# Reordering the prologue of a fused adaLN block: fewer products of zeros, statistics first, part of the normalisation on GpSimd

## The chip, the cores and the metric

The kernel runs on one core of a Trainium2 chip. The metric is the time of one execution on the device, in microseconds. The engines are TensorE (PE; its weight loads are PEld), VectorE (DVE), ScalarE (ACT), GpSimd (POOL) and SyncE (SP), which issues most DMAs.

## The reference

For 8 batches x of 1024 rows by 256 columns, in float32:

```python
mod = (_silu(L0_c) @ L0_wmod).reshape(8, 6, 1, -1)
sa, ca, ga, sb, cb, gb = (mod[:, i] for i in range(6))
ga = (2 * (ga >= 0) - 1) * jnp.maximum(jnp.abs(ga), 0.25)     # gb likewise
h = _layernorm(x) * (1 + ca) + sa
x = x + ga * attention(h)       # softmax((h * w_lhs) @ (h * w_rhs).T) @ h
h = _layernorm(x) * (1 + cb) + sb
x = x + gb * (relu(h @ W1 + b1) @ W2 + b2)
```

The weights are 256 by 1536 (wmod), 256 by 1024 (W1) and 1024 by 256 (W2). The scores of one batch are symmetric up to the two sides w_lhs and w_rhs, which the kernel folds into per-column scales and shifts.

## The kernel before, in words

A batch has eight row tiles of 128 (NT), in two halves g of four (TH). The program is one long list of instructions. Every engine runs its own part of the list strictly in the order in which it was written: the function pin() at the end ties each instruction to the one before it on its engine, so the order of the calls in the source is the order of the queues. Engines wait for each other through semaphores.

The prologue (lines 79 to 167, 923 to 1051) prepares batch 0. After it, the loop over batches and row tiles (from line 1135) interleaves attention of batch b with the feed-forward part of batch b-1. TensorE does nearly all of that.

In the prologue:

- Loads. c, the rows of x of batch 0 in four pieces of two tiles (load_x0), wmod in two pieces (its first 512 columns on ScalarE's queue, the other 1024 on SP's), w_lhs and w_rhs, the biases, and x of batch 1.
- warm(n), line 138: one product of zeros with n columns on TensorE. One of 512 columns stands ahead of the transposes of c, and two of 512 and one of 256 stand behind them.
- SiLU of c, lines 157 to 164: two small transposes into pt, exp(-c) on ScalarE (den), then three VectorE instructions that make scT.
- mod_rows(part, parts), line 185: product of scT and a stretch of wmod (pmr), copied to rows by ScalarE (L197). mod_rows(0, 2) makes shift and scale of the attention, mod_rows(2, 1) and mod_rows(5, 1) the two gates.
- columns(wv, NI), line 171: w_lhs and w_rhs as columns (pt_v, L175). make_sides, line 215, transposes shift and scale into columns (pmc, L206) and multiplies them with those of w (four small VectorE instructions, L218 and L221).
- prepare_stats, prepare_rstd, prepare_norm (lines 256 to 285): mean and variance of a tile (two VectorE instructions, L237 and L238), 1/sqrt as exp(-0.5 log) (two on ScalarE, L243 and L244, for a half), and x normalised into xg (VectorE for batch 0, L282, one instruction for each tile).
- prepare_turn(0, g), line 343: eight transposes on TensorE (pth, L355; four tiles into each of two PSUM tiles), from which lT and rT, the two sides with their scale and shift, are made: lT on VectorE for the first half (L359) and on ScalarE for the second (vector=False, L369), rT on ScalarE (L363). The pool ps_t has two PSUM buffers, used in turn by all transposes.
- direct(0, i, parts), line 397: scores of row tile i (psc, L405) with one half of the columns, copied to sc by ScalarE (L412). direct(0, 0) and direct(0, 1) start with the first half of the columns, which need rT of the first half alone.
- Then the gates (lines 943 to 953, eight VectorE instructions on 8 partitions), their way to DRAM (rows_d), the loads of W1 and W2 behind them on SP, first_rows (prow, L992), keep_rows (L1002), the gate's multiplication of xg (xg_half, L1020), maxima and mirrored score blocks (mirror_first, L444 and L445).

Before the change the calls stand in this order: statistics of half 0, its rstd, mod_rows(0, 2), columns, two tiles' statistics of half 1, normalisation of half 0, the other two tiles' statistics, make_sides, prepare_turn(0, 0), rstd of half 1, its normalisation, the gates' mod_rows, prepare_turn(0, 1), direct(0, 0), direct(0, 1).

Of the kernel before, what the change touches and what calls it, by code (L numbers as in the profile page):

```python
# [11 lines left out]
F32 = mybir.dt.float32  # L12
AF = mybir.ActivationFunctionType
ALU = mybir.AluOpType
# [3 lines left out]
P = 128  # L18
# [6 lines left out]
def adaln_block_kernel(  # L25
# [13 lines left out]
    nc = tc.nc  # L39
    B, S, D = x.shape  # L40
# [4 lines left out]
    HALF = 512  # L45
    TH = HALF // P
# [10 lines left out]
    ps_t = ctx.enter_context(tc.tile_pool(name="ps_t", bufs=2, space=PSUM))  # L57
# [37 lines left out]
    c_sb, b2_row = early_d[:B, 0], early_d[:B, 1]  # L95
# [36 lines left out]
    ident = const.tile([P, P], F32, name="ident")  # L132
# [5 lines left out]
    def warm(n):  # L138

        pw = ps_s.tile([P, HALF], F32, tag="s", name=f"pw_{n}")  # L140
        nc.tensor.matmul(pw[:, :n], lhsT=zeros[:, :P], rhs=zeros[:, :n], start=True, stop=True)
# [6 lines left out]
            name=nc.get_next_instruction_name(),  # L148
            engine=mybir.EngineType.Activation,
# [1 line left out]
    )  # L151

    warm(HALF)
    pt = ps_t.tile([P, HALF], F32, tag="t", name="pt_c")
    NC_ = ND * B
    for k in range(ND):
        nc.tensor.transpose(pt[:, ts(k, B)], c_sb[:, ts(k, P)], ident[:B, :B])
    scT = const.tile([P, ND, B], F32, name="scT")
    scf = scT.rearrange("p k b -> p (k b)")
    den = const.tile([P, NC_], F32, name="den")  # L160
    nc.scalar.activation(den, pt[:, :NC_], AF.Exp, scale=-1.0)
    nc.vector.tensor_scalar(den, den, 1.0, None, ALU.add)
    nc.vector.reciprocal(den, den)
    nc.vector.tensor_tensor(scf, pt[:, :NC_], den, ALU.mult)
    warm(HALF)
    warm(HALF)
    warm(D)

# [16 lines left out]
    def mod_rows(part, parts):  # L185

        pm = ps_a.tile([P, HALF], F32, tag="a", name=f"pmr_{part}")
        w = parts * D
        for k in range(ND):
            nc.tensor.matmul(  # L190
                pm[:B, :w],
                lhsT=scT[:, k, :],
                rhs=wm[:, k, ds(part * D, w)],
                start=(k == 0),
                stop=(k == ND - 1),
            )
        nc.scalar.copy(  # L197
            mod[:, part : part + parts, :].rearrange("b s d -> b (s d)"), pm[:B, :w]
        )
# [13 lines left out]
    side_col = lambda side, what, k, b: sides[:, side, what, k, b : b + 1]  # L213

    def make_sides():
        pc = mod_columns(0)
        for side in range(2):
            nc.vector.scalar_tensor_tensor(  # L218
                sides[:, side, 0], pc[:, 1], 1.0, w_cols(side), ALU.add, ALU.mult
            )  # L220
            nc.vector.tensor_tensor(sides[:, side, 1], pc[:, 0], w_cols(side), ALU.mult)  # L221
# [5 lines left out]
    def rows_tile(b):  # L227
        rows_t[b] = two.tile([P, 2, D], F32, tag="rows", name=f"rows_{b}")
        return rows_t[b]
# [5 lines left out]
    def stats(mv, t, src, name):  # L235
        st = work.tile([P, nc.vector.BN_STATS_DIM], F32, tag="st", name=f"st_{name}")
        nc.vector.bn_stats(st, src)  # L237
        nc.vector.bn_aggr(mv[:, t, :], st)  # L238
# [13 lines left out]
    def prepare_start(b):  # L252
        xg_t[b] = two.tile([P, NT, DX], F32, tag="xg", name=f"xg_{b}")
        nc.gpsimd.memset(xg_t[b][:, :, D : D + 1], 1.0)

    def prepare_stats(b, g, tiles=range(TH)):

        if tiles[0] == 0:
            mv = work.tile([P, TH, 2], F32, tag="mva", name=f"mva_{b}_{g}")
            pre[b, g] = [mv]  # L260
        mv = pre[b, g][0]
        for j in tiles:
            stats(mv, j, x_t[b, g][:, j, :], f"a{b}_{g}_{j}")

    def prepare_rstd(b, g):
        pre[b, g].append(rstd_of(pre[b, g][0], "ra", f"ra_{b}_{g}"))

    def prepare_norm(b, g):

        mv, r = pre.pop((b, g))  # L270
        if b > 0:
            shift = work.tile([P, TH], F32, tag="rs", name=f"rs_{b}_{g}")
            nc.vector.scalar_tensor_tensor(shift, mv[:, :, 0], -1.0, r, ALU.mult, ALU.mult)
        for j in range(TH):
            t = g * TH + j
            if b > 0:
                nc.scalar.activation(
                    xg_t[b][:, t, 0:D], x_tile(b, t), AF.Identity,
                    scale=r[:, j : j + 1], bias=shift[:, j : j + 1],
                )  # L280
                continue
            nc.vector.tensor_scalar(  # L282
                xg_t[b][:, t, 0:D], x_tile(b, t), mv[:, j, 0:1], r[:, j : j + 1],
                ALU.subtract, ALU.mult,
            )
# [57 lines left out]
    def prepare_turn(b, g, vector=True):  # L343

        xg, pts = xg_t[b], []
        lT = lT_t[b, g] = two.tile([P, ND, HALF], F32, tag="lT", name=f"lT_{b}_{g}", bufs=2)
        rT = rT_t[b, g] = two.tile([P, ND, HALF], F32, tag="rT", name=f"rT_{b}_{g}", bufs=2)
        rows = lambda T, k: T[:, k, :].rearrange("p (t a v) -> p t a v", a=NV, v=V)
        for k in range(ND):
            if b > 0:  # L350
                pt = pre[b, g][:, k]
            else:
                pt = ps_t.tile([P, HALF], F32, tag="t", name=f"pth_{b}_{g}_{k}")
                for j in range(TH):
                    nc.tensor.transpose(pt[:, ts(j, P)], xg[:, g * TH + j, ts(k, P)], ident)  # L355
                pt = pt.rearrange("p (t a v) -> p t a v", a=NV, v=V)
            pts.append(pt)
            if vector:
                nc.vector.tensor_scalar(  # L359
                    rows(lT, k), pt, side_col(0, 0, k, b), side_col(0, 1, k, b),  # L360
                    ALU.mult, ALU.add,
                )
            nc.scalar.activation(  # L363
                rows(rT, k), pt, AF.Identity,
                scale=side_col(1, 0, k, b), bias=side_col(1, 1, k, b),
            )
        if not vector:
            for k in range(ND):
                nc.scalar.activation(  # L369
                    rows(lT, k), pts[k], AF.Identity,  # L370
                    scale=side_col(0, 0, k, b), bias=side_col(0, 1, k, b),
                )

# [10 lines left out]
    def score_row(b, i):  # L386
        if b == 0:
            return first_scores()[:, i].rearrange("p (n v) -> p n v", v=V)
        return sc_t[b].rearrange("p i a j v -> p j (i a) v")[:, i]
# [6 lines left out]
    def direct(b, i, parts=range(S // HALF)):  # L396
        if i == 0 and parts[0] == 0:
            sc_t[b] = two.tile([P, NT, NV, NT, V], F32, tag="sc", name=f"sc_{b}", bufs=1)
        for n in parts:
            lo, hi = max(i * P, n * HALF), (n + 1) * HALF  # L400
            if lo >= hi:
                continue
            psc = ps_s.tile([P, HALF], F32, tag="s", name=f"psc_{b}_{i}_{n}")
            for k in range(ND):
                nc.tensor.matmul(  # L405
                    psc[:, : hi - lo],
                    lhsT=lT_t[b, i // TH][:, k, ts(i % TH, P)],
                    rhs=rT_t[b, n][:, k, lo - n * HALF : HALF],
                    start=(k == 0),
                    stop=(k == ND - 1),  # L410
                )
            nc.scalar.copy(  # L412
                score_row(b, i)[:, lo // V : hi // V, :],
                psc[:, : hi - lo].rearrange("p (n v) -> p n v", v=V),
            )
# [505 lines left out]


    prepare_start(0)
    prepare_stats(0, 0)
    prepare_rstd(0, 0)
    mod_rows(0, 2)
    columns(wv, NI)
    prepare_stats(0, 1, range(2))
    prepare_norm(0, 0)
    prepare_stats(0, 1, range(2, TH))  # L930
    make_sides()
    prepare_turn(0, 0)
    prepare_rstd(0, 1)
    prepare_norm(0, 1)
    mod_rows(2, 1)
    mod_rows(5, 1)
    prepare_turn(0, 1, vector=False)
    direct(0, 0, range(1))
    direct(0, 1, range(1))


# [11 lines left out]
    nc.vector.tensor_tensor(rows_sb[:, 3, :], gate[:, 1, :], b2_row, ALU.mult)  # L953


    rows_tile(0)
    rows_d = dram.tile([B, 4, D], F32, name="rows_d")
    nc.sync.dma_start(out=rows_d, in_=rows_sb)
# [369 lines left out]
    b = B - 1  # L1328
# [75 lines left out]
```

## Time and profile before

| what | value |
|---|---|
| runs | 776.5, 776.8, 777.04 us, median 776.8 |
| the profiled execution | 778.43 us |
| its span (first to last instruction) | 776.6 us |
| TensorE busy | 762.5 us, 98% of the span |
| VectorE, ScalarE, GpSimd busy | 74%, 47%, 69% |
| granted TensorE clock over the span | 1.0 |
| first 24 us: TensorE busy | 21.18 us |
| first 24 us: VectorE, ScalarE, GpSimd busy | 14.08, 9.88, 1.72 us |

The page lists the chain of work that ended last: followed back from the last instruction, at each step to what released it, or to the instruction before it on its engine. The same chain can be listed in order of time for a stretch. The timeline lists each instruction with start, duration, engine, line, the tile written and the tile read, and in square brackets how long its engine had been idle before it and which instruction ended that. A float32 product shows as two rows, one for each of two passes. DMA issues come with the time from issue to landing.

### The profile page before, as it was taken

To read this page: it belongs to the slowest core of one execution; us is meant where nothing else is said; L and a number is where in the kernel's file an instruction comes from. 1 tells how busy PE (TensorE), PEld (TensorE's weight loads), DVE (VectorE), ACT (ScalarE), POOL (GpSimd) and SP (SyncE) were. 2 spreads that over 40 slices of the span, in tenths; PEclk is the share of its full clock that TensorE was granted. 3 is DMA by queue.
4 is the path that set the end of the run, shared out by engine and by line. 5 is a ranking of instruction groups with operands and counts; after the bars stand their busy time and mean duration, and the time that the engine had idled before them with its cause. 6 is when DMAs were issued, how large, how long until landed. Compare 5 with 4: busy or idle time off the path is not lost.

```text
span 776.6 us, 11486 instructions
## 1 busy us (share of the span) xinstructions
PE 762.5 (98%) x3710; PEld 620.6 (80%) x3710; DVE 575.8 (74%) x1238; ACT 366.4 (47%) x671; POOL 534.0 (69%) x626
## 2 busy tenths in 40 slices
PE   8999999999999999999999999999999999999998
PEld 3576788788887888878887888878888788889886
DVE  6597879768796787957888677876879677594632
ACT  4464545535465355544546444553546535251511
POOL 0533895977949688586868778497694968559641
PEclk9999999999999999999999999999999999999999
DMA  5314434355344464434543544435444335232220
GB/s 190 124 28 149 123 103 119 122 167 169 95 128 126 130 177 113 144 104 125 169 126 116 150 149 129 110 121 177 139 121 125 107 122 170 58 103 86 81 82 27
DMA packets 106211, 95.18 MB, mean 123 GB/s; under 512 B 29700, under 2 KB 98848, under 8 KB 106152
## 3 DMA queue, kind: packets, MB, share of 16 engines
q1 hardware_dynamic: 98408, 85.81, 37.8%
q10 hardware_dynamic: 7744, 8.65, 3.5%
q8 instruction: 29, 0.48, 0.2%
q14 instruction: 30, 0.25, 0.1%
HBM read 50.62 MB, written 43.81 MB: 122 GB/s over the span
## 4 chain that ended last, share of the span: by engine, by line
PE 84%; DVE 10%; issue 2%; ACT 2%; POOL 1%; DMA 1%; SPq 0%; DVEq 0%; POOLq 0%
PE psc L405 14%; PE po L488 13%; PE pa L713 8%; PE pb L713 6%; PE yb L791 6%; PE ya L791 6%; PE pc L713 6%; PE yc L791 5%; PE pr L579 4%; PE pp L539 3%; PE py L896 3%; PE pq L579 3%; PE yd L791 3%; DVE pT L467 1%; DVE m L455 1%
## 5 line engine op out<-in xcount | busy, mean ns | idle before, releaser
L765 POOL TENSOR_TENSOR f<-f,kept 128x512 f32<-128x512 f32 x64 | 81.7, 1276 | 118.2 <-DVE f L764 89.6
L405 PE MATMUL psc<-rT,lT 128*128 128x512 f32 (+3 forms) x384 | 134.3, 486 | 0.0
L488 PE MATMUL po<-xg,pT 128*128 128x257 f32 x576 | 131.6, 380 | 0.0
L488 PEld LDWEIGHTS po<-xg,pT 128*128 128x128 f32 x576 | 108.8, 190 | 16.0 <-issue 1.0
L405 PEld LDWEIGHTS psc<-rT,lT 128*128 128x128 f32 x384 | 67.6, 190 | 38.1 <-issue 27.0
L412 ACT COPY sc<-psc 128x512 f32<-128x512 f32 (+3 forms) x96 | 44.8, 474 | 96.5 <-PE psc L405 96.5
L467 DVE TENSOR_TENSOR pT<-sc,pm 128x1024 f32<-128x1024 f32 x64 | 77.1, 1205 | 5.9 <-PE pm L460 5.8
L774 ACT ACTIVATE f<-f 128x512 f32<-128x512 f32 x64 | 40.4, 631 | 83.8 <-POOL f L765 83.8
L476 ACT ACTIVATE pT<-pT 128x1024 f32<-128x1024 f32 x64 | 67.0, 1047 | 26.4 <-DVE pT L467 26.4
L455 DVE TENSOR_REDUCE m<-sc 128x1 f32<-128x1024 f32 x64 | 77.1, 1205 | 0.0
L732 ACT COPY kept<-pa 128x512 f32<-128x512 f32 x64 | 37.4, 585 | 80.7 <-PE pa L713 80.7
L629 POOL TENSOR_TENSOR x<-x,rows 128x256 f32<-128x256 f32 x64 | 45.3, 740 | 37.4 <-ACT rows L1002 23.2
L713 PE MATMUL pb<-hs,w1s 128*128 128x256 f32 x256 | 67.1, 385 | 0.9 <-DVE f L750 0.6
L713 PE MATMUL pc<-hT,w 128*128 128x256 f32 x256 | 66.2, 381 | 0.0
L428 DVE STREAM_TRANSPOSE Tm<-sc 128x896 f32<-128x896 f32 (+6 forms) x49 | 34.7, 707 | 27.6 <-ACT sc L412 27.3
L713 PEld LDWEIGHTS pc<-hT,w 128*128 128x128 f32 x256 | 48.1, 190 | 7.7 <-ACT kept L732 1.4
L713 PEld LDWEIGHTS pb<-hs,w1s 128*128 128x128 f32 x256 | 45.5, 191 | 11.0 <-DVE f L750 4.6
L791 PE MATMUL yc<-f,w2s 128*128 128x256 f32 x224 | 52.1, 379 | 0.0
L791 PEld LDWEIGHTS yc<-f,w2s 128*128 128x128 f32 x224 | 41.5, 190 | 10.1 <-issue 2.9
L786 POOL TENSOR_TENSOR ft<-ft,f 128x256 f32<-128x256 f32 x56 | 41.9, 749 | 4.4
L785 POOL TENSOR_TENSOR ft<-ft,f 128x256 f32<-128x256 f32 x56 | 40.9, 730 | 4.4
L861 POOL TENSOR_TENSOR x<-x,Y 128x512 f32<-128x512 f32 x28 | 35.0, 1272 | 10.6 <-DMA Y<-D_y 10.6
(164 smaller groups left out, 1676.2 us busy)
## 6 DMA issues: line engine op xcount, KB each, us to landing
D_f<-T_f SPq DMA_DIRECT2D x60, 128.0 KB, 2.3
X_f<-D_f SPq DMA_DIRECT2D x15, 512.0 KB, 3.9
D_a<-T_a SPq DMA_DIRECT2D x56, 128.0 KB, 3.5
D_y<-T_y SPq DMA_DIRECT2D x56, 128.0 KB, 2.8
Y<-D_y SPq DMA_DIRECT2D x14, 512.0 KB, 3.9
out_dram<-x SPq DMA_DIRECT2D x14, 512.0 KB, 4.3
X_a<-D_a SPq DMA_DIRECT2D x13, 512.0 KB, 3.4
x<-in_L_attn_x_dram ACTq DMA_DIRECT2D x12, 512.0 KB, 3.8
```

Source lines behind the costliest of these rows:

```text
L405: nc.tensor.matmul(psc[:, : hi - lo], lhsT=lT_t[b, i // TH][:, k, ts(i % TH, P)], rhs=rT_t[b, n][:, k, lo - n * HALF : HALF], start=(k == ...
L412: nc.scalar.copy(score_row(b, i)[:, lo // V : hi // V, :], psc[:, : hi - lo].rearrange("p (n v) -> p n v", v=V),)
L455: nc.vector.tensor_reduce(m, score_row(b, i), AX.XY, ALU.max)
L467: nc.vector.tensor_tensor(pT.rearrange("p j (a v) -> p j a v", v=V), score_columns(b, i), pm[:, :P].rearrange("p (j a v) -> p j a v", j=1, ...
L476: nc.scalar.activation(pT_t[b, i], pT_t[b, i], AF.Exp)
L488: nc.tensor.matmul(po[:, : D + 1], lhsT=pT[:, t, :], rhs=xg_t[b][:, t, 0 : D + 1], start=(t == 0), stop=(t == NT - 1),)
L579: nc.tensor.matmul(out, lhsT=lhs[:, t, :], rhs=rhs[:, t, :], start=(t == 0), stop=(t == TH - 1),)
L629: queue.append(lambda: nc.gpsimd.tensor_tensor(out, in0, row, op))
L713: nc.tensor.matmul(out, lhsT=lhsT, rhs=rhs, start=True, stop=True)
L765: nc.gpsimd.tensor_tensor(f[:, c::NH, hi], f[:, c::NH, hi], kept[:, None, hi].to_broadcast([P, 2, H2]), ALU.add,)
L786: add(ft[:, 2, c], ft[:, 1, c], f[:, c + NH, lo], ALU.subtract)
L791: nc.tensor.matmul(out, lhsT=lhs(c), rhs=rhs(c), start=(c == 0), stop=(c == NH - 1))
```

## The change

The call of warm(512) behind the transposes of c is left out once (two of 512 and one of 256 become one of each). The three VectorE instructions of SiLU are put into a function, which is called behind the statistics of the first two tiles. Normalisation of batch 0 goes to GpSimd for every tile from the third on (t counts over all eight, so that is two tiles of the first half and all four of the second). The rstd and the normalisation of the second half stand ahead of prepare_turn(0, 0). direct(0, 0) with the first half of the columns stands ahead of prepare_turn(0, 1). The lT of the second half is made on VectorE and not on ScalarE, by the function left, which is called behind the gates. No load is moved.

```diff
     warm(HALF)
...
-    nc.vector.tensor_scalar(den, den, 1.0, None, ALU.add)
-    nc.vector.reciprocal(den, den)
-    nc.vector.tensor_tensor(scf, pt[:, :NC_], den, ALU.mult)
-    warm(HALF)
+
+    def silu():
+        nc.vector.tensor_scalar(den, den, 1.0, None, ALU.add)
+        nc.vector.reciprocal(den, den)
+        nc.vector.tensor_tensor(scf, pt_c[:, :NC_], den, ALU.mult)
+
     warm(HALF)
     warm(D)
...
-            nc.vector.tensor_scalar(
+            engine = nc.vector if t < TH // 2 else nc.gpsimd
+            engine.tensor_scalar(
                 xg_t[b][:, t, 0:D], x_tile(b, t), mv[:, j, 0:1], r[:, j : j + 1],
                 ALU.subtract, ALU.mult,
             )
...
-        if not vector:
+        def left():
             for k in range(ND):
-                nc.scalar.activation(
-                    rows(lT, k), pts[k], AF.Identity,
-                    scale=side_col(0, 0, k, b), bias=side_col(0, 1, k, b),
+                nc.vector.tensor_scalar(
+                    rows(lT, k), pts[k], side_col(0, 0, k, b), side_col(0, 1, k, b),
+                    ALU.mult, ALU.add,
                 )
+
+        return left
...
     prepare_start(0)
-    prepare_stats(0, 0)
+    prepare_stats(0, 0, range(2))
+    silu()
+    prepare_stats(0, 0, range(2, TH))
     prepare_rstd(0, 0)
     mod_rows(0, 2)
     columns(wv, NI)
...
     prepare_norm(0, 0)
     prepare_stats(0, 1, range(2, TH))
     make_sides()
-    prepare_turn(0, 0)
     prepare_rstd(0, 1)
     prepare_norm(0, 1)
+    prepare_turn(0, 0)
     mod_rows(2, 1)
     mod_rows(5, 1)
-    prepare_turn(0, 1, vector=False)
     direct(0, 0, range(1))
+    left = prepare_turn(0, 1, vector=False)
     direct(0, 1, range(1))
...
+    left()
     rows_tile(0)
     rows_d = dram.tile([B, 4, D], F32, name="rows_d")
     nc.sync.dma_start(out=rows_d, in_=rows_sb)
```

More of the change, by code (lines that the diff above doesn't have):

```diff
@@ L153, in adaln_block_kernel @@
     warm(HALF)
-    pt = ps_t.tile([P, HALF], F32, tag="t", name="pt_c")
+    pt_c = ps_t.tile([P, HALF], F32, tag="t", name="pt_c")
     NC_ = ND * B
     for k in range(ND):
-        nc.tensor.transpose(pt[:, ts(k, B)], c_sb[:, ts(k, P)], ident[:B, :B])
+        nc.tensor.transpose(pt_c[:, ts(k, B)], c_sb[:, ts(k, P)], ident[:B, :B])
     scT = const.tile([P, ND, B], F32, name="scT")
@@ L160, in adaln_block_kernel @@
     den = const.tile([P, NC_], F32, name="den")
-    nc.scalar.activation(den, pt[:, :NC_], AF.Exp, scale=-1.0)
-    nc.vector.tensor_scalar(den, den, 1.0, None, ALU.add)
-    nc.vector.reciprocal(den, den)
-    nc.vector.tensor_tensor(scf, pt[:, :NC_], den, ALU.mult)
-    warm(HALF)
+    nc.scalar.activation(den, pt_c[:, :NC_], AF.Exp, scale=-1.0)
+    def silu():
+        nc.vector.tensor_scalar(den, den, 1.0, None, ALU.add)
+        nc.vector.reciprocal(den, den)
+        nc.vector.tensor_tensor(scf, pt_c[:, :NC_], den, ALU.mult)
     warm(HALF)
```

## Prediction

> **What bounds the kernel now.** I read the page's span and its chain by engine first, then the chain of waits in order of time for the first 30 us, then the timeline of that stretch engine by engine, because the diff touches nothing that runs later.
>
> ```profile
> span 776.6 us, 11486 instructions
> ...
> PE 84%; DVE 10%; issue 2%; ACT 2%; POOL 1%; DMA 1%; SPq 0%; DVEq 0%; POOLq 0%
> ```
>
> TensorE carries 84% of the chain and its queue is in program order. So what the prologue saves in front of TensorE moves everything behind it by the same amount, and what it saves elsewhere is worth nothing. The chain at the start (start, duration, what):
>
> ```profile
> 1.45 2.08 PE pw L141 x2
> 3.53 0.31 PE pt_c L157 x2
> 3.84 4.03 PE pw L141 x6
> 7.87 1.83 PE pmr L190 x4
> ...
> 9.72 0.57 ACT early_b L197
> 10.30 0.06 ACT cols L175
> 10.36 0.40 PE pmc L206 x4
> 10.76 0.60 PE pth L355 x4
> ...
> 12.23 1.50 ACT rT L363 x2
> 13.73 0.19 ACT ra L243
> ...
> 14.19 0.42 DVE xg L282
> ...
> 14.66 1.74 PE pth L355 x8
> 16.39 3.01 PE psc L405 x8
> ```
>
> Three things are to be seen: products of zeros (pw) lie on the chain until 7.87; the second rstd (ra) and the second normalisation (xg) lie on it, queued on ScalarE behind rT; and the first scores (psc) begin at 16.39, after the transposes that wait for that normalisation. From 14.66 TensorE runs without a gap to 27.05. The loads of its weights show its speed:
>
> ```profile
> 6.49 0.34 PEld L141 LDWEIGHTS pw<-early_a 128*128 128x128 f32 x1 [0.52 <-issue]
> ...
> 7.28 0.19 PEld L141 LDWEIGHTS pw<-early_a 128*128 128x128 f32 x1 [0.45 <-issue]
> ```
>
> Loads at 4.78, 5.64 and 6.49 are 0.85 apart, the four pmr passes of 512 columns after 7.80 are 0.43 apart. TensorE doubles its speed between 6.49 and 7.28 (0.79 apart instead of 0.85, so near 7.2).
>
> **What the skill says.** "TensorE: Matmul & The Clock Gate", Part 1, says that the array runs at half speed until a free-running window of about 3.4 us has been busy, whatever the number of matmuls. The trace agrees: 0.85 against 0.43, and 7.2 is 3.4 after the zeros resume at 3.77. "GPSIMD Engine Reference", section 3.1, gives about 2.6 cycles an element for two inputs and 1.03 for short bodies with one. Two inputs agree here: 1272 ns for 512 elements and about 730 for 256 make 2.12 ns an element and 0.19 us fixed. One input is not in this trace. "PSUM — Partial Sum Buffer", section "PSUM bank collisions raise a hardware error", wants two engines kept apart on one bank; here rT (12.23) starts as lT on the same bank ends (12.20).
>
> **The change, part by part.** Times in us of the profiled execution; "was" is before.
>
> *One 512-column product of zeros less.* Two passes of 0.85 at half speed leave. The passes that remain start at about 3.93 and 4.78 (512 columns), 5.64 and 6.06 (256, half as long) and end at 6.49. The product pmr needs scT and its half of wmod. wmod is issued at 1.20 and takes 4.6: 5.8. scT is worked out next.
>
> *SiLU behind two tiles of statistics.* The first tiles of x land at 0.74+2.7=3.4, VectorE was idle until 4.09. A pair of statistics takes 0.53 (4.75 to 5.31), so two run from 3.45 to 4.5; SiLU took 0.66 (4.09 to 4.75), so scT is ready near 5.25, was 4.85. Both are before 6.49: the delay costs nothing, and it would cost only beyond 1.2. pmr therefore starts at 6.6, was 7.85. If the clock still rises at 7.2, 70% of its first pass runs slowly, and the four passes end at 7.33, 7.75, 8.18, 8.6. The copy L197 starts at 8.75, was 9.72: **0.95 to 1.0 gained**; the other quarter of a microsecond is the part of pmr that now runs cold. The chain L197, cols, pmc, sides keeps its lengths: pmc 9.4 (was 10.35), sides from 9.93.
>
> *Statistics in front of the sides.* On VectorE two more pairs (their tiles landed by 4.7) end at 6.3; rstd (ACT, 0.1+0.54) is ready at 7.1, was 7.6. The next two tiles of x land at 2.31+4.3=6.6, two pairs run to 7.7, two normalisations (0.32 each, was four) to 8.35, two pairs to 9.4. So VectorE is free 0.5 before sides, as before (0.5). lT starts at 10.44, was 11.38; 0.95 kept. The second rstd moves ahead of rT on ScalarE: it runs 9.5 to 10.05, in ScalarE's gap (it waits for lT until 11.3), so it delays nothing, and it is ready four microseconds before its old 14.15.
>
> *Six of eight tiles normalised on GpSimd.* The test is t < TH // 2 with t counting over both halves, so tiles 2 to 7 move. Nothing else is queued on GpSimd there (idle 2.3 to 25.5). The price of one is bounded below by the one-input rate, an estimate from the page named, 0.19+256x1.03/1.2 ns = 0.41; above by two passes of the two-input row, 2x0.74=1.48. I take 0.75. First two: from 7.1 to 8.6, wanted by the third transpose at about 9.95. Last four: from 10.1 to 13.1, wanted from 14.6 to 14.95. Both hidden. Cover is gone at 1.4 and 1.2 each; at 1.48 the last is ready at 16.0, 1.1 late. VectorE loses 0.32x6 of work, which was its part of the chain at 14.19.
>
> *First scores ahead of the later transposes.* The transposes of the first half run 9.74 to 11.05 (were 10.69 to 12.00). The two pmr of the other rows need the second part of wmod, 3.44+7.5=10.9, and run to 12.88. rT waits for both lT: 11.28 and 12.0, ending at 12.78. So psc of the first tile starts at 12.9 with TensorE nearly without a gap, and ends at 14.6. Then the eight transposes, 1.3 to 1.4 (were 1.74, the difference being waits for xg), to 15.95, then the 384-column psc (1.28) to 17.24, was 19.40: **2.15 gained**. So the former gap of 0.8 at 13.85 and 0.4 inside the transposes add to the first 0.95.
>
> *Does the next step follow?* prow needs the gates' rows (L943 to L953, 3.57 from 15.48 to 19.05). They now wait for ScalarE's copies behind rT, 12.8 to 13.45, and run 13.5 to 17.05: ready 0.2 before TensorE wants them. Their DMA to DRAM, and behind it rows, W1 and W2 on SP's queue, go out 2.1 earlier; no queue issues anything else in another order. rT of the second half runs 15.3 to 16.8, wanted at 18.1.
>
> *left() on VectorE.* Two 128x512 tiles of lT (0.73 each from L359) leave ScalarE and come to VectorE behind the gates, 17.05 to 18.6. VectorE was idle there for 3.86 us before xg_half, which waits for the rows copy (was 22.50+0.38, now 20.7). The two banks stay taken until 18.6; the mirrors ask for them at 21.5. Cost nothing; it would bite only 2 us later. ScalarE loses 1.45, off the chain.
>
> Sum: 2.15 off. The profiled execution took 778.43 with a span of 776.6, so 1.8 lies around the span; its span should become about 774.4. The shown runs have median 776.8, nearer the span, and the difference is applied to it: 776.8-2.15 = 774.65, given as 774.6. From 20 us on I find no step whose wait doesn't move with TensorE: ScalarE's wait at 27.05 and VectorE's chain at 42.6 to 48.5 have inputs that landed by 14 or come from the shifted order.
>
> **The rivals.** (1) *The clock rises a window later, or the modulation path is otherwise late.* The page calls the window free-running; if fewer zeros leave it short of busy, pmr runs all cold, 4x0.85 from 6.6 to 10.0, 1.4 later. Then 2.15-1.4 = 0.75 is left: 776.0. Against: TensorE stays busy from 3.77 through pmr. The GpSimd upper price gives 1.1 left, 775.7, in the same place. (2) *Slower: GpSimd becomes the bound.* It decides from 1.67 us a tile, where 7.1+6x1.67 = 17.1 is 2.15 after 14.95. At 2.4 a tile, twice a two-engine pass and more, the last is ready at 21.5: +6.6-2.15, 781.2. For it: no one-input arithmetic with two per-partition scalars in the trace. Against: it would be over three times the 256-element row of 0.73. (3) *The gain is given back later*, at the gates, left() or the mirrors, by a wait that this order leaves too tight; 0.2 us is the slack of prow. That ends near 776.8.
>
> **How the numbers follow.** Forecast 0.70, at 774.6, with 773.9 to 775.5 for it alone (GpSimd from 0.41 to 1.3, the clock up to 0.4 later, 0.5 between runs). Rival 1 has 0.15, rival 2 0.08, rival 3 0.07. A measurement here can tell about 0.2% from no change, 1.55 us. Rival 1 and half of 3 lie within it, so faster 0.75 (with rival 1's better half), same 0.16, slower 0.09. The range reaches to 776.5 to take in rival 1 and stops at 773.9, since TensorE's remaining gap in the prologue, 8.6 to 9.4, isn't touched.
>
> **What would show it.** Right: pmr near 6.6, first psc near 12.9, the rows copy near 20.3 to 20.7, everything after 25 moved by about 2.1. Wrong: transposes waiting for POOL; pmr passes 0.85 apart after 7.3; prow waiting for VectorE; mirrors waiting for left().

## The result, and the profile after

| | before | changed |
|---|---|---|
| median of 22 runs | 776.6 us (775.22 to 778.15) | 775.42 us (774.61 to 776.84) |
| ratio, 95% interval | | 0.9986 (0.998 to 0.9993) |
| profiled execution, its span | 778.43, 776.6 us | 775.09, 773.3 us |

The change makes the kernel faster by 0.14%, 1.1 us, with an interval from 0.5 to 1.55 us. The forecast was a time of 774.6, 2.15 us below before. The direction was right and the range (773.9 to 776.5) holds the time, but the gain is half of what was worked out, and it lies within the 0.2% that the prediction had called hard to tell from no change.

The chain of waits in order of time, changed kernel (start, duration, what), against the chain shown for before:

```profile
3.84 2.86 PE pw L141 x4
6.69 2.39 PE pmr L192 x4
...
9.11 0.57 ACT early_b L199
9.69 0.06 ACT cols L177
9.75 0.40 PE pmc L208 x4
10.15 0.60 PE pth L358 x4
...
10.78 0.82 DVE lT L362
11.60 4.31 POOL xg L285 x3
...
15.95 0.77 PE pth L358 x5
16.72 1.29 PE psc L410 x4
18.01 0.86 PE prow L1000 x2
```

Most of the forecast is there: one product of zeros less, pmr 1.2 earlier, rstd and its ScalarE queue gone from the chain. But where VectorE's normalisation stood, GpSimd's now stands, with 4.31 us. The timeline of GpSimd (start, duration, operation, and in brackets its own idle time before):

```profile
7.27 2.46 POOL L285 TENSOR_SCALAR xg<-x,mva,ra 128x256 f32<-128x256 f32 x2 [4.96 <-ACT ra L246]
10.39 5.51 POOL L285 TENSOR_SCALAR xg<-x,mva,ra 128x256 f32<-128x256 f32 x4 [0.66 <-ACT ra L246]
```

The view of line L285 has the single durations:

```profile
L285 POOL TENSOR_SCALAR xg<-x,mva,ra x6: 1220/1224/1906, 7.3 to 14.0; 128x256 f32<-128x256 f32 x6
L285 DVE TENSOR_SCALAR xg<-x,mva,ra x2: 382/454/525, 7.8 to 8.1; 128x256 f32<-128x256 f32 x2
```

In this view the three numbers are minimum, median and maximum in ns: a tile takes 1.22 us on GpSimd, and 1.9 in one case. The forecast had 0.75. TensorE pays for it:

```profile
13.21 1.98 PE L410 MATMUL psc<-rT,lT 128*128 128x512 f32 x4
15.03 0.49 PE L358 MATMUL pth<-ident,xg 128*128 128x128 f32 x3
15.95 0.77 PE L358 MATMUL pth<-ident,xg 128*128 128x128 f32 x5 [0.43 <-POOL xg L285]
```

The first scores do start three microseconds earlier than before. Three transposes follow, and the fourth waits for GpSimd's last tile. The product of the first row tile with xg (po, the end of the prologue) starts at 30.68 instead of 32.08.

The two spans differ by 3.3 us, far more than the medians. Only 1.4 of it lies in the prologue, as the next table shows; the rest comes and goes between executions.

### The profile page after: what moved, and what is told of

The parts are those of the page before. It is cut to its first block, busy times and chain, and to the rows that moved or that the text cites. A ratio compares the mean times of both kernels' runs of the same rounds, so it can differ in the third digit from the quotient of the medians.

```text
span 773.3 us, 11483 instructions
## 1 busy us (share of the span) xinstructions
PE 760.5 (98%) x3708; PEld 620.6 (80%) x3708; DVE 573.3 (74%) x1234; ACT 365.8 (47%) x669; POOL 541.5 (70%) x632
## 4 chain that ended last, share of the span: by engine, by line
PE 81%; DVE 11%; DMA 2%; ACT 2%; POOL 2%; issue 2%; SPq 1%; DVEq 0%; POOLq 0%
PE psc L410 14%; PE po L493 12%; PE pa L718 7%; PE pb L718 6%; PE yc L796 6%; PE ya L796 6%; PE yb L796 6%; PE pc L718 5%; PE pr L584 4%; PE py L901 3%; PE pq L584 3%; PE pp L544 3%; PE yd L796 3%; DVE pT L472 1%; DVE m L460 1%
## 5 line engine op out<-in xcount | busy, mean ns | idle before, releaser
L706 POOL TENSOR_TENSOR hs<-hT 128x256 f32<-128x256 f32 x16 | 11.6, 728 | 45.1 <-DVE hT L697 45.1
```

## The experiments

Theory: GpSimd's tiles are the missing part of the gain; the order of scores and transposes hides the rest of their time. Rivals: the rise of TensorE's clock; a gain that is given back later; parts of the change that are hidden anyway. Every run leaves a profile, in which po says how long the prologue took. All times in us; the clock's rise is the time from which the trace's record of the clock shows full speed (it has no entry ahead of that); pmr and first psc are the starts of their first weight loads; "rest" is the span minus the start of po. The experiments fall into three groups, beside which the kernel before had medians of 776.65 (no_pool, split, scores_back, warm_only), 776.96 (zeros_back, one_zero, silu_first, before_again) and 776.78 (after_again, split_again, split_gates, left_back). Times of different groups are therefore compared by the ratio and not by the median.

| kernel | clock's rise | pmr | first psc | po | rest | median | ratio to before, 95% interval |
|---|---|---|---|---|---|---|---|
| before | 7.20 | 7.80 | 16.12 | 32.08 | 744.6 | 776.6 | |
| before_again | 5.17 | 6.79 | 15.51 | 31.47 | 742.9 | 776.11 (one) | |
| changed | 7.79 | 6.62 | 13.20 | 30.68 | 742.6 | 775.42 | 0.9986 (0.998 to 0.9993) |
| after_again | 6.37 | 6.53 | 12.90 | 30.42 | 743.8 | 775.56 | 0.998 (0.9971 to 0.9988) |
| no_pool | 8.20 | 6.62 | 13.42 | 30.24 | 743.3 | 774.94 | 0.9972 (0.9959 to 0.9985) |
| split | 4.96 | 5.83 | 12.87 | 29.69 | 743.0 | 774.79 | 0.9978 (0.9969 to 0.9987) |
| split_again | 6.85 | 6.62 | 12.75 | 29.58 | 743.8 | 774.62 | 0.9973 (0.9961 to 0.9984) |
| split_gates | 5.71 | 6.20 | 12.68 | 29.51 | 742.9 | 774.74 | 0.9974 (0.9963 to 0.9984) |
| scores_back | 5.18 (half speed again from 12.01 to 15.42) | 6.24 | 16.03 | 31.98 | 743.1 | 777.7 | 1.0012 (1.0001 to 1.0023) |
| warm_only | 6.02 | 6.35 | 15.52 | 31.48 | 743.8 | 776.37 | 0.9993 (0.9984 to 1.0002) |
| zeros_back | 7.04 | 7.72 | 13.73 | 31.09 | 743.5 | 776.48 | 0.9994 (0.9986 to 1.0002) |
| one_zero | 8.74 | 5.60 | 13.17 | 30.52 | 743.2 | 776.52 | 0.9997 (0.9988 to 1.0005) |
| silu_first | 5.84 | 6.26 | 12.94 | 30.41 | 743.8 | 775.68 | 0.9983 (0.9977 to 0.999) |
| left_back | 7.57 | 6.62 | 13.09 | 30.54 | 743.9 | 775.81 | 0.9985 (0.9978 to 0.9993) |

**No tile on GpSimd.** Edit to the changed kernel:

```diff
-            engine = nc.vector if t < TH // 2 else nc.gpsimd
+            engine = nc.vector
...
-    prepare_norm(0, 1)
     prepare_turn(0, 0)
+    prepare_norm(0, 1)
```

> The change, but all eight tiles normalised on VectorE; the second half's four behind prepare_turn(0, 0). Theory (the six tiles on GpSimd, 1.22 us each, hold TensorE's later transposes by 0.7): VectorE has the four tiles ready near 13.7, TensorE asks for them at 14.6 to 15.0, so the first product po starts near 30.1 instead of 30.7, and the time is 0.5 to 0.7 below the changed kernel (0.7 to 0.9 of a per mille of the time). Rival (GpSimd's wait is paid anyway by what follows, the missing part of the forecast lies in the clock and at the batch boundaries): po at 30.7, same time as the changed kernel.

Measured: po 30.24, although the clock rose 0.4 later than in the changed kernel's profile; median 774.94. The timelines of VectorE and TensorE show the four tiles done in 1.38 us, in good time:

```profile
12.43 1.38 DVE L285 TENSOR_SCALAR xg<-x,mva,ra 128x256 f32<-128x256 f32 x4
...
13.42 1.98 PE L410 MATMUL psc<-rT,lT 128*128 128x512 f32 x4
...
15.24 1.04 PE L358 MATMUL pth<-ident,xg 128*128 128x128 f32 x8
```

The eight transposes now run in one piece of 1.04. VectorE has room for all of the normalisation once its last part stands behind lT. Six tiles on GpSimd are no gain over that: the ratio is 0.9972 against 0.9986 and 0.998 of the changed kernel, though the intervals overlap, and the clearer evidence is po.

**Four tiles on GpSimd, twice.** Tiles 2 to 5 on GpSimd, the last two on VectorE behind lT (prepare_norm takes the tiles as an argument, which isn't shown):

```diff
-            engine = nc.vector if t < TH // 2 else nc.gpsimd
+            engine = nc.gpsimd if 2 <= t < 6 else nc.vector
...
-    prepare_norm(0, 1)
+    prepare_norm(0, 1, range(2))
     prepare_turn(0, 0)
+    prepare_norm(0, 1, range(2, TH))
```

> The change with four tiles on GpSimd instead of six: tiles 2 to 5 on GpSimd, 6 and 7 on VectorE behind prepare_turn(0, 0). Theory: GpSimd ready at 12.9, VectorE at 13.0, no wait at the later transposes; po near 30.1, equal to the kernel without GpSimd within 0.1. Rival: po at 30.7, as the changed kernel.

> Four tiles on GpSimd instead of six, once more. Theory: no wait for GpSimd in front of the later transposes, po 0.5 to 0.9 before that of the changed kernel at a like clock (29.7 with an early rise, 30.2 with a late one), time 0.5 to 0.8 below it (ratio to before near 0.9977). Rival: the same time as the changed kernel.

Measured: po 29.69 and 29.58, medians 774.79 and 774.62. The first po is 0.4 earlier than expected, with the earliest rise of all (4.96). The second run lay beside after_again, the changed kernel run again on the same chip: po 0.84 earlier at nearly the same rise of the clock (6.85 and 6.37), of which 0.15 lies ahead of the first scores and 0.7 at the later transposes. The median is 0.94 lower; the intervals of the two ratios overlap, so that po carries the argument. So six tiles instead of four cost 0.8 to 0.9 us. TensorE's timeline in split_again has no wait left between the first transposes and the first scores of the second half:

```profile
9.61 1.37 PE L360 MATMUL pth<-ident,xg 128*128 128x128 f32 x8
10.93 1.89 PE L192 MATMUL pmr<-wm,scT 128*8 128x256 f32 x8
12.75 1.98 PE L412 MATMUL psc<-rT,lT 128*128 128x512 f32 x4
14.57 1.04 PE L360 MATMUL pth<-ident,xg 128*128 128x128 f32 x8
15.45 1.46 PE L412 MATMUL psc<-rT,lT 128*128 128x384 f32 x4
```

This kernel is 2.1 us (0.27%, interval 0.16 to 0.39%) faster than before, what had been forecast for the change.

**The changed kernel again.**

> The changed kernel once more, beside the next two. Theory: another phase of the clock, but po stays between 30.4 and 30.7, since GpSimd's six tiles and not pmr set the later transposes: the wait for GpSimd in front of them is there again, longer when the clock rises early. Time 1.1 below before. Rival (the clock is what kept the gain small): with an early rise po near 29.9 and no wait for GpSimd.

Measured: the clock rose 1.4 earlier than in its first profile, pmc came 0.66 earlier (9.07 against 9.73), and po only 0.26 (30.42). GpSimd takes up the rest: its second group starts at 10.72 here (10.39 in the first profile), because the statistics on VectorE that it needs end 0.33 later, and the wait of the fourth transpose is there again, in TensorE's timeline:

```profile
14.72 0.49 PE L358 MATMUL pth<-ident,xg 128*128 128x128 f32 x3
15.69 0.77 PE L358 MATMUL pth<-ident,xg 128*128 128x128 f32 x5 [0.48 <-POOL xg L285]
```

The rival that the clock kept the gain small (po near 29.9) falls.

**Scores behind the transposes again.**

```diff
-    direct(0, 0, range(1))
     left = prepare_turn(0, 1, vector=False)
+    direct(0, 0, range(1))
     direct(0, 1, range(1))
```

> The change with the first scores behind the later transposes again. Theory (the early scores cover GpSimd's tiles): TensorE waits for GpSimd from 13.2 to 15.9 with nothing else to do, and then runs 0.4 of transposes and 3.0 of scores: prow near 19.5, po near 32.2, the time of before or slightly above (776.5 to 777). Rival (the order of scores and transposes is worth nothing): po at 30.7.

Measured: po 31.98, 0.5 later than before at the same rise of the clock (5.18; before_again 5.17 and 31.47), and 1.3 to 1.6 later than the changed kernel; median 777.7. TensorE's timeline:

```profile
9.15 0.55 PE L358 MATMUL pth<-ident,xg 128*128 128x128 f32 x3
10.40 0.76 PE L358 MATMUL pth<-ident,xg 128*128 128x128 f32 x5 [0.70 <-POOL xg L285]
11.56 3.19 PE L192 MATMUL pmr<-wm,scT 128*8 128x256 f32 x8 [0.40 <-DMA wm<-in_L_wmod_dram]
14.68 1.62 PE L358 MATMUL pth<-ident,xg 128*128 128x128 f32 x8
16.14 3.17 PE L410 MATMUL psc<-rT,lT 128*128 128x512 f32 x8
```

In this profile, with its early rise, even the first two GpSimd tiles hold the first transposes, by 0.70.

po is close to the expected 32.2, but not quite by the expected course. From 13.2 on TensorE isn't idle: the gates' pmr take 3.19 and not 1.89, because the clock falls to half speed for 3.4 us. In this view each line has a stretch, its length, the busy time of PE, PEld, DVE, ACT and POOL (with the number of instructions), and then the granted clock, followed by two numbers for the DMAs:

```profile
11.00:12.00 1.00, 0.60 (x4) 0.19 (x3) 1.00 (x2) 0.39 (x1) 1.00 (x2) 1.00 1.09 380
12.00:13.00 1.00, 1.00 (x4) 0.40 (x3) 0.29 (x1) 1.00 (x2) 1.00 (x1) 0.50 0.83 269
14.00:15.00 1.00, 1.00 (x4) 0.32 (x3) 0.00 (x0) 0.21 (x1) 1.00 (x2) 0.50 0.00 0
```

GpSimd's last tile ended at 15.48, and of the long wait that was expected for it only 0.35 is left, at the weight loads of the last transposes:

```profile
15.53 0.53 PEld L358 LDWEIGHTS pth<-ident,xg 128*128 128x128 f32 x5 [0.35 <-POOL xg L285]
```

The scores follow the end of that tile by 0.66, as they do in the changed kernel (15.89 and 16.55). So, as an estimate from these numbers, the fall of the clock cost nothing here: at full clock TensorE would have waited longer for the same tile. But the slow products end so near to it that this one profile doesn't separate the two causes.

The times of all executions say more. In six of the 13 executions the mean granted clock was 0.998 or less (one stretch of 3.4 us at half speed lowers it by 0.002); their median is 778.81. The other seven have 776.8. The kernel before has 776.65 beside them, and none of its 36 executions had so low a clock; nor had any of the 22 of the changed kernel. So without the early scores the rest of the change gains nothing that can be told, and it is slower than before only where the clock falls.

**One product of zeros less, and nothing else.** Edit to the kernel before:

```diff
-    warm(HALF)
     warm(HALF)
     warm(D)
```

> The kernel before with one 512-column product of zeros less and nothing else. Theory: pmr starts 1.2 earlier, part of it at half speed, and all behind it follows by 0.65 (clock up at 7.8) to 0.95 (at 7.2): po near 31.1 to 31.4, time 775.7 to 776.0. Rival (the statistics and normalisation on VectorE set the start of the transposes, so that the zeros were hidden): po at 32.1, 776.6.

Measured: pmr at 6.35 with a rise at 6.02, and po at 31.48, where before_again has 31.47 with pmr at 6.79. The median is 0.3 lower than before and the interval holds no change. The chain of waits of warm_only shows why:

```profile
8.03 1.27 DVE xg L281 x4
9.29 0.35 DVE st_a L236
9.66 0.18 DVE mva L237
9.84 0.32 DVE st_a L236
...
10.29 0.16 DVE sides L217
...
11.51 0.82 DVE lT L358
12.36 0.78 ACT rT L362
```

In the order of before, sides can't start ahead of 10.28, when VectorE is through with statistics and normalisation. With a late clock TensorE arrives there at 10.88 (first profile of before), and zeros are on the chain; with an early one VectorE sets the time, and they are hidden. The rival was right for early clocks. The 0.65 to 0.95 that the theory gives for a late clock were not seen, since this kernel's one profile had no late rise.

**The product of zeros put back into the changed kernel.**

```diff
     warm(HALF)
+    warm(HALF)
     warm(D)
```

> The change with the left-out 512-column product of zeros put back. Theory (the product lies on the chain when the clock rises late, and is hidden when it rises early): pmr at 7.8 if the clock rises near 7.2, po 0.6 to 0.7 later than the changed kernel (31.3); with a rise near 5, pmr at 6.3 to 6.4 and po 0.3 later. Time 0.3 to 0.7 above the changed kernel, 775.7 to 776.1. Rival (zeros always hidden by the statistics and GpSimd): po 30.7, 775.4.

Measured: with a rise at 7.04, pmr 7.72 and po 31.09, 0.4 to 0.7 later than the two profiles of the changed kernel, where 0.6 to 0.7 was expected. Median 776.48; of the ratio's gain little is left (0.9994, and its interval includes 1), which is 0.6 us above the changed kernel. Leaving the zeros out of the old order gave 0.3 us, within the noise. That they cost more in the changed order fits VectorE, which is free at 9.4 here and not at 10.3, but no profile of this kernel has an early clock, so it isn't shown.

**Only 256 columns of zeros behind the transposes of c.**

```diff
-    warm(HALF)
     warm(D)
```

> The change with the second 512-column product of zeros left out too, so that only the one of 256 columns follows the transposes of c. Theory (the zeros that remain are there to raise the clock, and TensorE must wait for wmod until 5.8 anyway): TensorE idles from 4.8 to 5.8, and where the clock isn't up, pmr takes 3.4 instead of 1.7 to 2.4: po between 30.3 (clock up early) and 31.7 (a window later), time within 0.5 of the changed kernel. Rival (zeros are waste): pmr at 5.9 and 0.7 faster, 774.7.

Measured: pmr starts at 5.6 and takes twice as long, the clock rises at 8.74:

```profile
3.76 1.22 PE L141 MATMUL pw<-early_a 128*128 128x256 f32 x2
5.63 3.40 PE L191 MATMUL pmr<-wm,scT 128*8 128x512 f32 x4 [0.65 <-DVE st_a L238]
8.97 0.22 PE L175 MATMUL pt_v<-ident,early_d 4*128 4x4 f32 x1
```

po at 30.52 is that of the changed kernel, but the ratio is 0.9997 instead of 0.9986. That is 0.9 us, more than was expected and more than this prologue explains. Against silu_first, run beside it, the median is 0.84 higher. One profile has one rise of the clock; with other phases po may lie later, but this wasn't seen. The rival, 0.7 faster, falls; what the remaining zeros are worth and where stays open.

**SiLU first.**

```diff
-    prepare_stats(0, 0, range(2))
     silu()
-    prepare_stats(0, 0, range(2, TH))
+    prepare_stats(0, 0)
```

> The change with SiLU ahead of the statistics, as before. Theory (scT is ready well ahead of pmr in both orders, statistics are not what lT waits for): pmr, psc and po where they are in the changed kernel at the same clock, 775.4 within the noise. Rival (the statistics in front are the gain): rstd ready 0.4 to 0.5 later, GpSimd's tiles and po later by as much, 775.9.

Measured: po 30.41 with a rise at 5.84, median 775.68: the changed kernel within 0.3. This part is worth nothing that can be told.

**lT of the second half on ScalarE.**

```diff
-        def left():
-            for k in range(ND):
-                nc.vector.tensor_scalar(
-                    rows(lT, k), pts[k], side_col(0, 0, k, b), side_col(0, 1, k, b),
-                    ALU.mult, ALU.add,
-                )
-
-        return left
+        if not vector:
+            for k in range(ND):
+                nc.scalar.activation(
+                    rows(lT, k), pts[k], AF.Identity,
+                    scale=side_col(0, 0, k, b), bias=side_col(0, 1, k, b),
+                )
...
-    left = prepare_turn(0, 1, vector=False)
+    prepare_turn(0, 1, vector=False)
...
-    left()
```

> The change with lT of the second half on ScalarE again, ahead of the score copies. Theory: ScalarE has 1.45 of room there (the copy of the 384-column scores then starts near 19.2, and TensorE wants its PSUM buffer at 20.4): po and time as in the changed kernel, 775.4. Rival (this move is part of the gain): 0.3 to 1.0 slower.

Measured: po 30.54, median 775.81 (0.9985 against 0.998 beside it, intervals overlapping). ScalarE's timeline has the two tiles, and then the copy of scores with time to spare:

```profile
17.52 1.45 ACT L372 ACTIVATE lT<-pth,sides 128x512 f32<-128x512 f32 x2
18.84 0.49 ACT L415 COPY sc<-psc 128x384 f32<-128x384 f32 x1
20.48 0.59 ACT L415 COPY sc<-psc 128x512 f32<-128x512 f32 x1 [1.15 <-PE psc L408]
```

**The gates' columns of wmod first**, on top of four tiles on GpSimd:

```diff
-    nc.sync.dma_start(out=wm[:, :, 2 * D : 6 * D], in_=wmod_v[:, :, 2 * D : 6 * D])
+    for lo_, hi_ in ((2, 3), (5, 6), (3, 5)):
+        nc.sync.dma_start(
+            out=wm[:, :, lo_ * D : hi_ * D], in_=wmod_v[:, :, lo_ * D : hi_ * D]
+        )
```

> The same with four tiles on GpSimd, and the second part of wmod loaded in three pieces, the columns of the two gates first. Theory (what holds the first scores there is the gates' pmr, which wait for wmod until 11.05): the gates' pmr start at 10.3 instead of 11.05 when the clock rises early, and the first scores then wait for rT: 0.4 earlier, po 29.3. With a late rise nothing, since pmr of the gates is then not waiting. Rival (two more DMAs on SP's queue push x and the biases back): first scores not earlier, time up to 0.5 above that of the kernel with four tiles.

Measured: the gates' pmr start at 10.86, not at 10.3, although the clock rose at 5.71; the first transposes end late, behind GpSimd's second tile:

```profile
9.09 0.55 PE L363 MATMUL pth<-ident,xg 128*128 128x128 f32 x3
9.90 1.03 PE L363 MATMUL pth<-ident,xg 128*128 128x128 f32 x5 [0.27 <-POOL xg L290]
10.86 1.89 PE L195 MATMUL pmr<-wm,scT 128*8 128x256 f32 x8
```

po 29.51 and 774.74: no gain that can be told. Neither theory nor rival came true: the load was no longer what was waited for.

**The kernel before, once more.**

> The kernel before, once more, for another phase of the clock. Theory: the rise of the clock falls anywhere in 4.8 to 8.2, and po moves with it: 32.1 at 7.2, about 31.4 to 31.6 for a rise near 5. And the stall in front of the pm product near 414 isn't there in every execution: the distance from po to that product, 381.9 in the first profile, is 0.3 to 1.0 shorter. Rival: both as in the first profile.

Measured: po 31.47 with a rise at 5.17, as expected, and a span of 774.3. The column "rest" gives the reason for the misleading spans: from po to the end all fourteen profiles take 742.6 to 744.6, and the first profile of before has the longest. One stall in it lies inside a later batch. The chain of that profile around 405 us:

```profile
404.96 2.26 DMA D_y<-T_y
...
407.98 0.67 DVE T_a L317
408.65 1.10 DVE pT L467
```

The same place in the chain of the changed kernel:

```profile
404.75 0.02 DVEq L752
...
404.99 0.67 DVE T_a L320
405.66 1.11 DVE pT L472
```

In the one, T_a waits for a DMA that still reads the buffer it goes into; in the other the DMA is done. From po to the product pm behind that place it is 381.9 in the first profile of before and 380.5 in the second, 1.4 shorter, where 0.3 to 1.0 was expected. All the others lie from 380.3 to 381.9, whatever was changed; left_back has 381.9 too, without that DMA in its chain. Such waits come and go between executions, by 2.0 in sum; why a DMA is late in one execution wasn't tried.

## Why the prediction was half right

*Zeros.* "0.95 to 1.0 gained" up to L197 was 0.6 in the profile (9.11 against 9.72): the clock rose at 7.79 and not at 7.2, so pmr took 2.39 and not 2.0. The mechanism was right. That the rise at 7.2 came 3.4 after the zeros resumed was chance: in before_again it came 1.4 after. What the forecast missed is that the profile of before had a late rise itself. With a rise at 5.17 the kernel before reaches po at 31.47, and its zeros are hidden behind VectorE.

*SiLU and statistics.* Costing nothing and giving nothing at the sides: right (silu_first).

*GpSimd.* This step failed: "I take 0.75 ... Both hidden. Cover is gone at 1.4 and 1.2 each." A tile takes 1.22, and the last 1.3 to 1.9 in the two profiles, while VectorE's gate instructions run beside it; that these are the reason wasn't tried by itself. The last tile was ready at 15.9 and not at 13.1, and TensorE waited for it (0.43 idle on the row of the products, 0.67 by its weight loads). At 1.22 for all four it would have been ready at 15.27, just ahead of the 15.52 at which TensorE asked: no margin was left, and the slow last tile made the wait; in after_again the later start (10.72) did. Four tiles instead of six give 0.8 to 0.9 back, and none on GpSimd has a ratio as low. The upper bound of 1.48 held for most tiles but not for the last, and the prediction had its consequence, "1.1 left, 775.7", among the rivals; the value taken was the wrong one. The estimate of 0.41 from "GPSIMD Engine Reference", section 3.1, is a third of what this instruction takes, and the two-input row of 0.73 is no upper bound for it.

*Scores ahead.* Right in its start (13.2 and 12.9 against 12.9), and without it the rest gains nothing that can be told (scores_back). No run moves the scores alone, so what they would give by themselves is open.

*Gates, left(), mirrors.* Right: no wait appeared at prow, and the change of engine for lT is worth nothing that can be told (left_back).

*Nothing given back later.* No sign against it: "rest" is the same for all kernels within its scatter, which is 2.0 us, and the medians differ by about as much as po does (1.1 us against 1.05 to 1.4).

The sum: 2.15 less 0.8 to 0.9 for GpSimd is 1.3, and the difference of 1.1 between the medians is within its interval of that. The rival with the upper price of GpSimd came true, not the one with the clock, though the clock did rise later in the profile. That 775.42 still lies in the part of the range meant for the forecast alone (up to 775.5, for at most 1.3 a tile) is luck in part: the last four tiles took 1.38 each on average.

## What to carry to other kernels

Moving work to an idle engine is worth something only where the engine it leaves was late; here VectorE had room, once the order was changed. Before taking a value between two bounds for an operation that the trace doesn't show, ask at what value the cover is gone, and use the answer: the prediction had it (1.2, between the bounds of 0.41 and 1.48) and still costed the step at nothing. When an edit makes a kernel slower, look at the clock over the stretch before putting the time down to the wait that was expected. And a span of one profile shows a change of a microsecond only up to a milestone behind it; take the rest from several profiles.

## What the runs showed of the hardware

- TENSOR_SCALAR with two per-partition scalars (subtract, multiply) of 128x256 float32 took 1.21 to 1.28 us on GpSimd in 43 of the 54 tiles of these profiles. That is 1.7 times the two-input TENSOR_TENSOR of that size (0.73); on VectorE it mostly took 0.38 to 0.41. The other eleven tiles, 1.30 to 1.91, ran while VectorE normalised or made the gates, and VectorE's own tiles took up to 0.64 beside GpSimd (after_again).
- The rise of TensorE's clock lay anywhere from 4.96 to 8.74 in fourteen profiles, and from 4.96 to 8.20 without the kernel with the fewest zeros: 3.2 us, nearly the window of 3.4 that "TensorE: Matmul & The Clock Gate", Part 1, calls free-running. The traces agree: the stretches of full speed in the record of the clock, and the one of half speed between two of them, last 3.413, 6.827, 761.172, 764.585, 767.999 or 771.412 us, whole multiples of 3.413. In the kernel before, the rise moved po by 0.6.
- The clock fell in one prologue, that of scores_back, after a window of 3.41 us (8.59 to 12.01, counted from the rise) in which TensorE was busy for 2.10. In split_again such a window near the end (768.02 to 771.43) had 2.10 too, and the clock stayed up, so the busy time alone gives no rule here.
